# The two ends of a selective-scan layer: where its first rows wait and where its last projection stands

## The chip, the core and the metric

The program runs on one core of one Trainium2 chip. The metric is the device time of one execution in microseconds (us). The core's engines are named as the profile names them: PE (TensorE matmul), PEld (its weight loads), DVE (VectorE), ACT (ScalarE), POOL (GpSimd) and SP (SyncE, which here only issues DMAs). Each runs its own list of instructions in order and waits on the others by semaphores.

## The reference, cut to what matters

Four layers work on `x` of 3 x 256 x 48 x 48 (2304 tokens an image). Layer 0 holds attention, layers 1 and 2 are 3x3 convolutions, layer 3 is a selective scan along the tokens:

```python
# layer 3; b: image, l: token, d: 512 inner channels, n: 16 states
dt = softplus(x_dbl[..., :16] @ dt_proj_w.T + dt_proj_b)
def step(hst, inp):                       # one token
    dt_t, B_t, C_t, u_t = inp
    hst = hst * exp(dt_t[:, :, None] * A) + dt_t[:, :, None] * B_t[:, None, :] * u_t[:, :, None]
    return hst, einsum('bdn,bn->bd', hst, C_t)
y = (ys + u * D_param) * silu(z)
out = einsum('bld,cd->blc', y, out_proj_w)
x = x + out
```

The change touches the passage from layer 2 into layer 3 and the first and the last step of layer 3. What is computed stays the same.

## The kernel before

**Passage from layer 2.** Layers 1 and 2 work in half images (`halves`, twelve of them). A half's products of 3x3 kernels are L1546 (`ps_c`), and DVE writes their sums into `xs[b]`, the image in SBUF (L1573 to L1576). `store_tokens` (L1630) then copies a finished half into token order on ACT (L1642, two copies of 128 x 1152) into a staging tile, and one DMA (L1649) sends it to `xd[b]` in DRAM, whence layer 3 fetches it in chunks. For all halves but the last one the staging tile is `xpad` and SP issues the DMA. For the last, image 0's second half, it is a tile of the pool `vp` (`vt`) and ACT's queue issues it. Image 0 is last in `ORDER`, so layer 3 reads these tokens only in its last chunks. After the last half DVE also runs the group norm's last links (`norm_steps`, L180 to L192, L162, L216 to L218, L1614, L1615, with two small PE products and one POOL instruction between).

**Where layer 3's tiles lie.** When layer 2 ends, its pools are closed and layer 3's tiles take their places from the bottom up: first `wp` (five tiles of 6,144 bytes a partition, and `diag`), then `scn` in the order in which its tiles are first asked for: `dtr` (two buffers of 6,144), `dtur` (two of 3,104), `dtuq`, `hs` (three of 12,416), `hc` (two of 12,288). So `dtr` lies where the end of layer 2's weights (`u`, 36,864 bytes) and its product sums (`tmp`) were, and `hs` where `xpad`, `wc`, `we` and `vt` were. A tile's first use waits for what last used its place.

**The scan.** A chunk is 384 tokens of one image; there are 18. A chunk has eight steps (`m` in 0..3, `h` in 0..1), so there are 144 steps. A step has eight parts, and a part `(g, q)` is one ACT exponential of 128 x 384 (`decay`, L1809) into one of three PSUM slots and one DVE scan of 128 x 385 (`scan`, L1817) over a slice of the state tile `hs`. `decay` runs three parts ahead of `scan`. The scan's inputs are written into `hs` by `fill`: the upper half (q 0, 1) by DVE from the PSUM tile `ps_r` (`fill_upper`, L1765), which PE makes from `dtu` (`spread_pe`, L1730); the lower half (q 2, 3) by POOL (L1783, and one part by L1779) from rows that DMAs replicate (`dtur`, `dtuq`; `spread`, L1714, and `spread_second`, L1722). The rows that `decay` reads (`dtr`) come by `spread` as well. `fill(0)` writes step 0's upper half and a part of step 1's. After the eight parts of step s follow `fill(s+1)`, POOL's product with C over all of `hs` (`times_c`, L1834, result `hc`), and PE's sum over states of the step before (`add_states(s-1)`, L1851, with one product of `diag` and `u` at L1846 when h is 0). For the last step DVE makes the product with C in two halves (L1828).

**What stands beside the parts.** `run(at, j, place)` calls the other stages of the chunks before and after at fixed parts: `project_x` (L1263) for the next chunk after part 3 of step 0, `take_x` (L1269) on ACT at parts 5 and 6, `taps` (L1273, sixteen PE instructions for two m) at parts 6 and 7, `take_u` (L1281) on ACT in step 1. `gate` (L1858, DVE) multiplies a finished `y` with silu(z), three steps late. `project_y` is the output projection: one product of `ident` and the residual `ot` (L1372) and four of `w("out")` and `sz` (L1374) for each half of the channels. `store` copies it out of PSUM on ACT (L1384) and sends it (L1385).

**Busywork.** `keep_busy(src, times)` (L1333) issues that many PE products of 128 x 128 x 128 (L1336, two instructions each) whose results nobody reads, into the unused columns of the current `ps_r` tile. The table `busy` names the parts that get some, none of them in steps with m = 0 or m = 1.

**Order.** `keep_order` fixes the order of PE, DVE, ACT and POOL from `mark` on as the code has it. SP's order, and the order of what stands ahead of `mark`, come from the planner that places ready instructions.

After the last step the code of before does the whole of the last chunk's output: `residual`, `project_y` for m 0 to 2, `add_states(end)`, `gate`, `project_y` for m = 3 and `store`, for each half of the channels.

Of the kernel before, what the change touches and what calls it, by code (L numbers as in the profile page):

```python
# [9 lines left out]
F32 = mybir.dt.float32  # L10
# [6 lines left out]
P = 128  # L17
# [3 lines left out]
CT = 2  # L21
# [4 lines left out]
CH = 384  # L26
NCH = N // CH
NT = N // P
TW = HW // 4

PW = TW + 1
HR = HW // 2
HN = HR * TW
TAPS = 9
EXPERTS = 8
DI = 4
# [37 lines left out]
ORDER = (2, 1, 0)  # L74
# [10 lines left out]
def net(  # L85
# [21 lines left out]
    nc = tc.nc  # L107
# [44 lines left out]
    xs = {}  # L152
# [3 lines left out]
    xd = [dram.tile([P, CT, N], F32, name=f"xd{b}", bufs=1) for b in range(B)]  # L156
# [224 lines left out]
    with ExitStack() as l0:  # L381
# [36 lines left out]
        with ExitStack() as p1:  # L418
# [15 lines left out]
            for b in ORDER:  # L434
# [3 lines left out]
                for ct in range(CT):  # L438
                    for j in range(parts):
                        at = slice(j * N // parts, (j + 1) * N // parts)  # L440
                        queue = nc.scalar if b == ORDER[0] and ct else nc.sync
# [93 lines left out]
        with ExitStack() as p2:  # L535
# [9 lines left out]
            for i in range(NB):  # L545
# [399 lines left out]
                vt = vpool.tile([P, NT, 384], F32, name="vt")  # L945
# [101 lines left out]
        i = NB - 1  # L1047
        mark = listed[-1]
        chunks = [(b, c) for b in ORDER for c in range(NCH)]
# [15 lines left out]
        for n, b in enumerate(ORDER):  # L1065
# [11 lines left out]
            for c in range(NCH):  # L1077
# [7 lines left out]
                if b == 0 and c == 3:  # L1085
                    vp = late_pool("vp", 2, last_pools)
                    pad = late_pool("pad", stack=last_pools)
# [20 lines left out]
    rooms, w3v, chunks, stored = {}, {}, {}, set()  # L1108
# [224 lines left out]
    def keep_busy(src, times):  # L1333

        for i in range(times if spread_tiles else 0):
            nc.tensor.matmul(  # L1336
                spread_tiles[-1][:, i % 2, CH:], ident, src, start=True, stop=True
            )
# [30 lines left out]
    def project_y(k, mo, lo=0, hi=DI, into=None):  # L1369
        if lo == 0:  # L1370
            k.y_out[mo] = bank[mo] if into is None else into
            nc.tensor.matmul(k.y_out[mo], ident, k.ot[:, mo, :], start=True, stop=False)  # L1372
        for m in range(lo, hi):
            nc.tensor.matmul(  # L1374
                k.y_out[mo], w("out", m * 256 + mo * P, P), k.sz[:, m, :],
                start=False, stop=m == DI - 1,
            )

    def residual(k):
        k.ot = room(k, "ot")  # L1380
        nc.sync.dma_start(k.ot, xd[k.b][:, :, k.c * CH : (k.c + 1) * CH])

    def store(k, mo):
        nc.scalar.copy(k.ot[:, mo, :], k.y_out[mo])  # L1384
        nc.sync.dma_start(  # L1385
            out[k.b, mo * P : (mo + 1) * P, k.c * CH : (k.c + 1) * CH], k.ot[:, mo, :]
        )
# [148 lines left out]
    with ExitStack() as l1:  # L1536
# [88 lines left out]
        def between():  # L1625
            next(pending, None)
            if at_unit >= 4:
                next(early, None)

        def store_tokens(b, h):  # L1630


            last = (b, h) == (ORDER[-1], 1)
            if last:
                t = vp.tile([P, 6, CT, (HR + 2) * TW], F32, name="vt")
                t = t.rearrange("p i t n -> p (i t n)")
            else:
                t = pad.tile([P, 4, CT * (HR + 2) * PW + 2], F32, name="xpad")
                t = t.rearrange("p j n -> p (j n)")
            t = t[:, : CT * 4 * HN].rearrange("p (t n) -> p t n", t=CT)  # L1640
            for ct in range(CT):
                nc.scalar.copy(  # L1642
                    t[:, ct, :].rearrange("p (n j) -> p j n", j=4),
                    xs[b][:, ct, :].rearrange("p (j n) -> p j n", j=4)[
                        :, :, h * HN : (h + 1) * HN
                    ],
                )
            queue = nc.scalar if last else nc.sync
            queue.dma_start(xd[b][:, :, h * 4 * HN : (h + 1) * 4 * HN], t)  # L1649
            stored.add((b, h))  # L1650

        vt = first_v
        behind, pending = None, iter(())
        for n, (k, h) in enumerate(halves):
            layer, b = units[k]
# [13 lines left out]
            vt = ahead  # L1669
# [9 lines left out]
            pass  # L1679
        for _ in early:  # L1680
            pass

    last_pools.close()

# [4 lines left out]
    with ExitStack() as l3:  # L1689
# [2 lines left out]
        psr = l3.enter_context(tc.tile_pool(name="psr", bufs=1, space=PSUM))  # L1692
        psy = l3.enter_context(tc.tile_pool(name="psy", bufs=1, space=PSUM))

        scn = l3.enter_context(tc.tile_pool(name="scn", bufs=2, reuse_waits="tile"))
        for name in ("u", "dtu", "bc0", "bc1", "sz"):
            rooms[name].append(wp.tile([P, 4, CH], F32, name=name))
# [19 lines left out]
        def spread_second(k, m):  # L1717

            t = scn.tile([P, 4 + CH], F32, name="dtuq", bufs=1)[:, 2 : 2 + CH]
            for i in range(4):  # L1720
                r = slice(32 * i, 32 * i + 32)
                nc.sync.dma_start(t[r], k.dtud[m & 2][:32, m & 1, :])  # L1722
            k.second[m] = t

        def spread_pe(k, m):

            t = psr.tile([P, 2, 512], F32, name="ps_r")
            for q in range(2):
                r = slice(32 * q, 32 * q + 32)
                nc.tensor.matmul(  # L1730
                    t[:, q, :CH], rep[r].rearrange("p r d -> p (r d)"), k.dtu[r, m, :],
                    start=True, stop=True,
                )
            k.ps = t
            lent[0] = t[:, 1, :CH]
            spread_tiles[:] = [t]


        steps = [(at, m, h) for at in range(len(todo)) for m in range(DI) for h in range(2)]
        tiles = {}  # L1740
        state = {}
        busy = {(2, 0, 3): 4, (2, 1, 1): 3, (2, 1, 2): 3, (2, 1, 3): 3, (2, 1, 5): 3,
                (3, 0, 0): 3, (3, 0, 1): 3, (3, 0, 2): 2}
# [77 lines left out]
        def times_c(s):  # L1821
            at, m, h = steps[s]
            cb = chunks[at].bc[1][:, 2 * h : 2 * h + 2, :].unsqueeze(2)
            hc = scn.tile([P, 2, 4, CH], F32, name="hc")
            if s == len(steps) - 1:

                for g in range(2):
                    nc.vector.tensor_tensor(  # L1828
                        hc[:, g], tiles[s][:, g, :, 1:],
                        cb[:, g].broadcast_to([P, 4, CH]), ALU.mult,  # L1830
                    )
                tiles[s] = hc
                return
            nc.gpsimd.tensor_tensor(  # L1834
                hc, tiles[s][:, :, :, 1:], cb.broadcast_to([P, 2, 4, CH]), ALU.mult
            )
            tiles[s] = hc
# [18 lines left out]
        def gate(at, m):  # L1856
            k = chunks[at]
            nc.vector.tensor_tensor(k.sz[:, m, :], k.y_ps[:, :CH], k.sz[:, m, :], ALU.mult)  # L1858

        mark = listed[-1]  # L1860
        last = len(todo) - 1
        k = chunks[0]
        k.rows = {0: spread(k, 0)}
        spread_second(k, 0)
        spread_pe(k, 0)
        first_states(0)
        fill(0)
# [2 lines left out]
        for s, (at, m, h) in enumerate(steps):  # L1870
            if m == 0 and h == 1 and at + 2 <= last:
                fetch(at + 2)
            for part in range(8):
                j = 4 * m + 2 * h + part // 4
                scan(s, part)
                decay(8 * s + part + 3)
                if (m, h, part) in busy:
                    g, q = parts_of_step[part]
                    keep_busy(tiles[s][:, g, q, 1 : P + 1], busy[m, h, part])
                if part == 0 and h == 0:  # L1880
                    c, n = (at, m + 1) if m + 1 < DI else (at + 1, 0)
                    if c <= last:
                        rows = getattr(chunks[c], "rows", {})
                        chunks[c].rows = {**rows, n: spread(chunks[c], n)}
                if part == 0 and h == 1 and s + 1 < len(steps):
                    spread_second(chunks[steps[s + 1][0]], steps[s + 1][1])
                if part == 4 and s + 1 < len(steps):
                    first_states(s + 1)
                if part % 4 == 0:
                    run(at, j, BEGIN)  # L1890
                if part % 4 == 1:
                    run(at, j, MID)
                if part % 4 == 2:
                    run(at, j, DONE)
                if h == 1 and part == 7 and s >= 3:
                    gate(*steps[s - 3][:2])
                if part % 4 == 3:
                    run(at, j, LATE)
                if part == 3:
                    run(at, j, PE_)  # L1900
            if s + 1 < len(steps):
                fill(s + 1)
            last_states(s)
            times_c(s)
            run(at, 4 * m + 2 * h + 1, PE_)
            if s >= 1:
                add_states(s - 1)

            if h == 0 and s + 2 < len(steps):
                spread_pe(chunks[steps[s + 2][0]], steps[s + 2][1])  # L1910

        end = len(steps) - 1
        k = chunks[last]
        residual(k)
        for mo in range(2):
            project_y(k, mo, 0, DI - 1)
        add_states(end)
        gate(*steps[end][:2])
        for mo in range(2):
            project_y(k, mo, DI - 1, DI)  # L1920
            store(k, mo)
        keep_order(tc, listed, mark)
    late_pools.close()

# [111 lines left out]
```

## Time and profile before

| | us |
|---|---|
| median of the runs (3373.8 to 3378.72) | 3374.56 |
| the profiled execution's own time | 3369.03 |
| its span, first to last instruction | 3367.3 |
| layer 3's scans, first start to last end | 2013.78 to 3344.6 |
| DVE busy in the span | 2899.6 (86%) |
| PE busy | 3151.7 (94%) |
| ACT busy | 2375.1 (71%) |
| POOL busy | 1335.3 (40%) |

The page averages over four layers with different limits, so the stretches around 2000 to 2035 us and 3330 to 3367 us, which the change touches, are to be read by themselves in the timeline. A line of the timeline gives start, duration, engine, line, operation and tiles; in brackets stands the engine's idle time before it and what ended it. PE's busy time is modelled and is not PE at its peak. "PEclk" is the TensorE clock that was granted, as a share of full speed; it was 0.982 over the span and is either 1 or 0.5 in any stretch that is short enough.

### The profile page before, as it was taken

How to read it: one execution, taken by the hardware profiler on the slowest of the kernel's cores; microseconds unless marked ns; L12 is line 12 of the kernel's file. 1: busy time of each engine (PE TensorE's matmuls, PEld its weight loads, DVE VectorE, ACT ScalarE, POOL GpSimd, SP SyncE). 2: the span in 40 equal slices, each digit the busy share in tenths (PEclk: the TensorE clock that was granted, in tenths of full speed). 3: DMA queues.
4: the chain of work that ended last, by engine and by line, in shares of the span. 5: the costliest groups of instructions: out<-in, count | busy, mean ns of one | idle time of the engine just before them, and what ended most of it. 6: DMA issues, size and time to landing. Idle time of an engine off the chain costs nothing.

```text
span 3367.3 us, 54979 instructions
## 1 busy us (share of the span) xinstructions
PE 3151.7 (94%) x21314; PEld 1586.5 (47%) x21314; DVE 2899.6 (86%) x3302; ACT 2375.1 (71%) x3596; POOL 1335.3 (40%) x457
## 2 busy tenths in 40 slices
PE   7999999999999999979999988999999999999985
PEld 4334343452333434547777764444444444444442
DVE  4799989959988997379976459999999999999997
ACT  3688888838888886332233548888888888888874
POOL 0000000000000000220000009999999999999997
PEclk9999999999999999989999999999999999999998
DMA  4000000010000002566611044555545555555552
GB/s 174 23 8 10 8 8 6 8 46 4 8 7 8 10 8 71 193 210 214 218 38 38 19 120 107 125 127 129 143 123 141 133 129 123 130 130 134 135 131 56
DMA packets 182165, 290.84 MB, mean 86 GB/s; under 512 B 34738, under 2 KB 148466, under 8 KB 179971
## 3 DMA queue, kind: packets, MB, share of 16 engines
q1 hardware_dynamic: 168658, 267.15, 29.6%
q10 hardware_dynamic: 13232, 20.06, 1.8%
q8 instruction: 169, 2.77, 0.4%
q14 instruction: 106, 0.86, 0.1%
HBM read 236.24 MB, written 50.64 MB: 85 GB/s over the span
## 4 chain that ended last, share of the span: by engine, by line
PE 52%; DVE 32%; ACT 7%; DMA 4%; issue 4%; SPq 1%; POOL 0%; ACTq 0%; DVEq 0%; POOLq 0%
DVE hs L1817 21%; PE ps_s L638 16%; PE acc L651 14%; PE ps_c L1546 8%; DVE hs L1765 3%; DVE u L296 2%; PE ps_y L462 2%; PE ps_m L665 2%; ACT ps_da L1809 2%; PE ps_s L1031 2%; PE ps_m L711 1%; PE acc L529 1%; PE ps_s L518 1%; DVE ps_g L1343 1%; DMA dtr<-dtd 1%
## 5 line engine op out<-in xcount | busy, mean ns | idle before, releaser
L642 ACT ACTIVATE pt<-ps_s 128x1024 f32<-128x1024 f32 x972 | 942.4, 1022 | 154.8 <-PE ps_s L638 142.1
L1817 DVE TENSOR_TENSOR_SCAN hs<-ps_da,hs 128x385 f32<-128x385 f32 x1152 | 1002.6, 936 | 5.1 <-ACT ps_da L1809 2.4
L857 DVE TENSOR_TENSOR part<-part,pt 128x2048 f32<-128x2048 f32 x396 | 906.6, 2289 | 41.2 <-ACT pt L642 18.5
L1809 ACT ACTIVATE ps_da<-dtr,u 128x384 f32<-128x384 f32 x1152 | 656.3, 582 | 191.3 <-DVE hs L1817 182.7
L164 POOL TENSOR_TENSOR rstd<-ve,mhalf 128x2 f32<-128x2 f32 (+1 forms) x26 | 16.3, 629 | 1473.4 <-DVE ve L162 1473.4
L638 PE MATMUL ps_s<-q,kt 32*128 32x512 f32 (+1 forms) x4320 | 576.4, 592 | 0.1
L651 PE MATMUL acc<-pt,vt 128*32 128x512 f32 (+1 forms) x4320 | 520.9, 561 | 0.2
L1546 PE MATMUL ps_c<-vt,u 128*128 128x288 f32 x1728 | 429.4, 409 | 21.0 <-DVE u L263 21.0
L1834 POOL TENSOR_TENSOR hc<-hs,x 128x3072 f32<-128x3072 f32 x72 | 405.2, 5628 | 30.8 <-DVE hs L1817 26.0
L1834 POOL TENSOR_TENSOR hc<-hs,bc 128x3072 f32<-128x3072 f32 x71 | 400.1, 5635 | 24.7 <-DVE hs L1817 23.0
L1546 PEld LDWEIGHTS ps_c<-vt,u 128*128 128x128 f32 x1728 | 328.9, 191 | 116.6 <-issue 19.8
L638 PEld LDWEIGHTS ps_s<-q,kt 32*128 32x128 f32 x4320 | 195.3, 183 | 199.1 <-issue 120.2
L651 PEld LDWEIGHTS acc<-pt,vt 128*32 128x32 f32 x4320 | 94.4, 108 | 353.4 <-issue 326.7
L1851 PE MATMUL ps_y<-hc,u 128*32 128x384 f32 x2304 | 228.1, 516 | 2.8 <-POOL hc L1834 2.8
L1273 PE MATMUL ps_g<-u 128*128 128x384 f32 x576 | 196.2, 494 | 23.4 <-ACT u L1269 23.4
L1783 POOL TENSOR_TENSOR hs<-dtur,x 128x1536 f32<-128x1536 f32 x72 | 209.0, 2903 | 8.3 <-DMA dtur<-dtud 8.3
L1783 POOL TENSOR_TENSOR hs<-dtur,bc 128x1536 f32<-128x1536 f32 x72 | 209.3, 2907 | 1.3 <-DMA dtuq<-dtud 0.9
L1273 PEld LDWEIGHTS ps_g<-u 128*128 128x128 f32 x576 | 108.8, 191 | 107.7 <-ACT u L1269 34.6
L1336 PE MATMUL ps_r<-hs,ident 128*128 128x128 f32 x864 | 130.9, 292 | 27.3 <-DVE hs L1817 27.2
L1336 PEld LDWEIGHTS ps_r<-hs,ident 128*128 128x128 f32 x864 | 107.6, 192 | 80.8 <-DVE hs L1817 63.0
L1851 PEld LDWEIGHTS ps_y<-hc,u 128*32 128x32 f32 x2304 | 62.0, 112 | 144.5 <-issue 130.4
L1562 ACT COPY cb<-ps_c 128x288 f32<-128x288 f32 x48 | 19.1, 398 | 154.5 <-PE ps_c L1546 140.4
(266 smaller groups left out, 4051.0 us busy)
## 6 DMA issues: line engine op xcount, KB each, us to landing
wconv<-in_we SPq DMA_DIRECT2D x144, 384.0 KB, 4.2
dtr<-dtd SPq DMA_DIRECT2D x288, 192.0 KB, 3.9
dtur<-dtud SPq DMA_DIRECT2D x288, 96.0 KB, 4.3
wconv<-xd SPq DMA_DIRECT2D x36, 384.0 KB, 3.7
x<-bcd SPq DMA_DIRECT2D x72, 192.0 KB, 5.1
dtd<-x SPq DMA_DIRECT2D x36, 384.0 KB, 2.9
dtuq<-dtud SPq DMA_DIRECT2D x288, 48.0 KB, 2.0
bc<-bcd SPq DMA_DIRECT2D x72, 192.0 KB, 4.8
```

Source lines behind the costliest of these rows:

```text
L638: nc.tensor.matmul(s[:, j, cols], kt[r, mt * P : (mt + 1) * P], q[r, :n], start=True, stop=True,)
L642: nc.scalar.activation(p[:, h0 : h0 + 2, :], s, AF.Exp)
L651: nc.tensor.matmul(acc[h * HD : (h + 1) * HD, :n], vt[:, mt, g * P + h * HD : g * P + (h + 1) * HD], p[:, h, cols], start=mt == 0, stop=mt ...
L857: ): nc.vector.tensor_tensor(part, first, p, ALU.add)
L1273: nc.tensor.matmul(bank[m % 2], w3v["taps"][:, m, tap, :], w3v["xi"][:, m % 3, tap : tap + CH], start=tap == 0, stop=tap == DCONV - 1,)
L1336: nc.tensor.matmul(spread_tiles[-1][:, i % 2, CH:], ident, src, start=True, stop=True)
L1546: nc.tensor.matmul(pc[:, :HN], u[:, i, dy, ct, m * P : (m + 1) * P], vt[:, i, ct, dy * TW : dy * TW + HN], start=ct == 0 and dy == 0, stop ...
L1783: nc.gpsimd.tensor_tensor(states(s)[:, :, 2:4, 1:], chunks[at].rows[m][1].unsqueeze(1).broadcast_to([P, 2, 2, CH]), b_rows(s, 0, 2), ALU.mult,
L1809: nc.scalar.activation(slots[n % 3][:, 1 : CH + 1], chunks[at].rows[m][0][:, q, :], AF.Exp, scale=amat[:, col : col + 1],)
L1817: nc.vector.tensor_tensor_scan(b, slots[(8 * s + part) % 3][:, : CH + 1], b, 0.0, ALU.mult, ALU.add)
L1834: nc.gpsimd.tensor_tensor(hc, tiles[s][:, :, :, 1:], cb.broadcast_to([P, 2, 4, CH]), ALU.mult)
L1851: nc.tensor.matmul(k.y_ps[32 * q : 32 * q + 32, :CH], fold, hc[:, g, q, :], start=False, stop=h == 1 and g == 1,)
```

## The change

Six edits, all in layer 3 and in the passage into it:

- The last half's tokens are copied on ACT in four pieces (768, 384, 384 and 768 elements a partition) into the rooms `ot` (two) and `sq`, which the scan needs only later. Four DMAs on SP send them, placed in the code after `spread(k, 0)` and `spread_second(k, 0)` of the first chunk. The staging tile in `vp` and the DMA on ACT's queue are gone.
- `hc` gets a pool of its own, `hcp`, opened ahead of `scn`. By the sizes above, `hc` then lies over layer 2's `tmp` and the end of `u`, `dtr` and `dtur` over `xpad`, `wc`, `we` and the first `vt`, and `hs` over the two `vt` and image 0 (`x0`).
- Step 0 gets three `keep_busy` products in each of parts 1 to 4; the last step gets three in each of parts 4 to 7.
- In the last step `project_y` for m = 0, 1 stands at part 0, `gate` of m = 2 and `project_y` of m = 2 at part 3 (the gate stood at part 7 before); `residual` stands at part 0 of the step before.
- After the last step only `add_states`, `gate` and `project_y` of m = 3 remain, and both stores.
- The second store's copy runs on DVE, the first one's stays on ACT.

```diff
-    def store(k, mo):
-        nc.scalar.copy(k.ot[:, mo, :], k.y_out[mo])
+    def store(k, mo, copy=nc.scalar.copy):
+        copy(k.ot[:, mo, :], k.y_out[mo])
...
+        late_stores = []
+
         def store_tokens(b, h):
-            last = (b, h) == (ORDER[-1], 1)
-            if last:
-                t = vp.tile([P, 6, CT, (HR + 2) * TW], F32, name="vt")
-                t = t.rearrange("p i t n -> p (i t n)")
-            else:
-                t = pad.tile([P, 4, CT * (HR + 2) * PW + 2], F32, name="xpad")
-                t = t.rearrange("p j n -> p (j n)")
+            if (b, h) == (ORDER[-1], 1):
+                a, c = rooms["ot"]
+                d = rooms["sq"][0]
+                at = h * HN
+                for ct, lo, hi, t in (
+                    (0, 0, 192, a.rearrange("p t n -> p (t n)")),
+                    (0, 192, HN, c[:, 0, :]),
+                    (1, 0, 96, c[:, 1, :]),
+                    (1, 96, HN, d.rearrange("p t n -> p (t n)")),
+                ):
+                    nc.scalar.copy(
+                        t.rearrange("p (n j) -> p j n", j=4),
+                        xs[b][:, ct, :].rearrange("p (j n) -> p j n", j=4)[
+                            :, :, at + lo : at + hi
+                        ],
+                    )
+                    late_stores.append((xd[b][:, ct, 4 * (at + lo) : 4 * (at + hi)], t))
+                return
+            t = pad.tile([P, 4, CT * (HR + 2) * PW + 2], F32, name="xpad")
+            t = t.rearrange("p j n -> p (j n)")
...
-            queue = nc.scalar if last else nc.sync
-            queue.dma_start(xd[b][:, :, h * 4 * HN : (h + 1) * 4 * HN], t)
+            nc.sync.dma_start(xd[b][:, :, h * 4 * HN : (h + 1) * 4 * HN], t)
...
+        hcp = l3.enter_context(tc.tile_pool(name="hcp", bufs=2, reuse_waits="tile"))
         scn = l3.enter_context(tc.tile_pool(name="scn", bufs=2, reuse_waits="tile"))
...
-            hc = scn.tile([P, 2, 4, CH], F32, name="hc")
+            hc = hcp.tile([P, 2, 4, CH], F32, name="hc")
...
+        end = len(steps) - 1
         k = chunks[0]
         k.rows = {0: spread(k, 0)}
         spread_second(k, 0)
+        for dst, src in late_stores:
+            nc.sync.dma_start(dst, src)
         spread_pe(k, 0)
         first_states(0)
         fill(0)
...
-                if (m, h, part) in busy:
+                n = busy.get((m, h, part), 0)
+                if (s == 0 and 1 <= part <= 4) or (s == end and part >= 4):
+                    n = 3
+                if n:
                     g, q = parts_of_step[part]
-                    keep_busy(tiles[s][:, g, q, 1 : P + 1], busy[m, h, part])
+                    keep_busy(tiles[s][:, g, q, 1 : P + 1], n)
+                if s == end and part == 0:
+                    for mo in range(2):
+                        project_y(chunks[at], mo, 0, 2)
+                if s == end and part == 3:
+                    gate(at, DI - 2)
+                    for mo in range(2):
+                        project_y(chunks[at], mo, 2, DI - 1)
+                if s == end - 1 and part == 0:
+                    residual(chunks[at])
...
-                if h == 1 and part == 7 and s >= 3:
+                if h == 1 and part == 7 and 3 <= s < end:
                     gate(*steps[s - 3][:2])
...
-        end = len(steps) - 1
         k = chunks[last]
-        residual(k)
-        for mo in range(2):
-            project_y(k, mo, 0, DI - 1)
         add_states(end)
         gate(*steps[end][:2])
         for mo in range(2):
             project_y(k, mo, DI - 1, DI)
-            store(k, mo)
+        for mo in range(2):
+            store(k, mo, (nc.scalar.copy, nc.vector.tensor_copy)[mo])
```

More of the change, by code (lines that the diff above doesn't have):

```diff
@@ L1681, in net @@
             pass
+        stored.add((ORDER[-1], 1))
     last_pools.close()
```

## The prediction

> **What bounds the kernel now.** I read the page first, then the timeline around the first and the last scan, then the clock in windows. In layer 3, the last third of the span, DVE sets the pace:
>
> ```profile
> L1817 DVE TENSOR_TENSOR_SCAN hs<-ps_da,hs 128x385 f32<-128x385 f32 x1152 | 1002.6, 936 | 5.1 <-ACT ps_da L1809 2.4
> ...
> L1834 POOL TENSOR_TENSOR hc<-hs,x 128x3072 f32<-128x3072 f32 x72 | 405.2, 5628 | 30.8 <-DVE hs L1817 26.0
> ```
>
> The scans idle 5.1 us in all, so a step that starts earlier stays earlier: what is won at the first step should reach the end. From the first scan at 2013.78 to the last one's end at 3344.56 a step takes 1330.8 / 144 = 9.24 us. In the middle, then, there is nothing to win; the two ends are read by themselves. The first (timeline):
>
> ```profile
> 2005.17 7.97 SPq L1714 DMA_DIRECT2D dtur<-dtud  x4
> ...
> 2006.08 0.60 ACTq L1649 DMA_DIRECT2D xd<-vt  x1
> ...
> 2008.33 1.76 DVE L1765 TENSOR_TENSOR hs<-ps_r,x 128x1536 f32<-128x1536 f32 x1
> 2009.15 1.28 ACT L1809 ACT_TABLE_LOAD   x1 [2.23 <-DMA dtr<-dtd]
> ...
> 2012.91 0.96 DVE L1765 TENSOR_TENSOR hs<-ps_r,x 128x768 f32<-128x768 f32 x1 [2.82 <-DMA xd<-vt]
> ...
> 2018.10 3.51 DVE L1817 TENSOR_TENSOR_SCAN hs<-ps_da,hs 128x385 f32<-128x385 f32 x4 [0.82 <-POOL hs L1783]
> ...
> 2020.99 8.08 PE L1273 MATMUL ps_g<-u 128*128 128x384 f32 x16 [12.79 <-ACT u L1269]
> ...
> 2030.20 0.96 DVE L1817 TENSOR_TENSOR_SCAN hs<-ps_da,hs 128x385 f32<-128x385 f32 x1 [1.64 <-ACT ps_da L1809]
> ```
>
> To be seen: DVE and the fourth `dtur` issue wait until the staged tokens have landed (2012.8); ACT waits for `dtr`, POOL for `dtur`. Then `taps` run 8.08 us on a slow PE, ACT's `take_u` stands behind them, `decay` behind `take_u`, and step 1's last scan waits 1.64 us. Step 1 ends at 2031.16. The other end:
>
> ```profile
> 3336.64 2.39 PE L1851 MATMUL ps_y<-hc,u 128*32 128x384 f32 x16 [2.82 <-POOL hc L1834]
> ...
> 3344.93 4.21 DVE L1828 TENSOR_TENSOR hc<-hs,bc 128x1536 f32<-128x1536 f32 x2
> ...
> 3346.64 2.79 PE L1851 MATMUL ps_y<-hc,u 128*32 128x384 f32 x16
> ...
> 3349.36 1.58 PE L1372 MATMUL ps_g<-wconv,ident 128*128 128x384 f32 x2
> ...
> 3356.96 0.56 DVE L1858 TENSOR_TENSOR sz<-ps_y,sz 128x384 f32<-128x384 f32 x1 [7.82 <-PE ps_y L1851]
> ```
>
> DVE is done at 3349.14; PE alone holds the end until 3356.96. And the clock, in windows (busy us and instructions of PE, PEld, DVE, ACT, POOL; then PEclk, the DMA share, GB/s):
>
> ```profile
> 2013.80:2021.00 7.20, 0.01 (x1) 0.01 (x1) 6.38 (x9) 4.11 (x9) 5.84 (x3) 0.50 0.81 196
> 2021.00:2026.30 5.30, 5.30 (x9) 2.88 (x10) 5.30 (x8) 3.19 (x7) 5.29 (x2) 0.50 0.20 48
> ...
> 3339.10:3345.00 5.90, 0.00 (x0) 0.00 (x0) 5.90 (x9) 2.47 (x5) 5.90 (x2) 0.50 0.00 1
> 3345.00:3350.70 5.70, 5.63 (x20) 1.94 (x21) 4.14 (x3) 0.00 (x0) 0.85 (x1) 0.50 0.01 3
> 3350.70:3357.00 6.30, 6.19 (x31) 2.89 (x29) 0.04 (x1) 0.00 (x0) 0.00 (x0) 1.00 0.00 0
> ```
>
> PE idles ahead of both ends and then works 5.3 and 5.7 us at half clock.
>
> [...]
>
> **Part by part, the start.** The two ACT copies took 2.27 us each. The first half's run beside the products, as now. Behind the last sum (2003.75) stand two pieces, 384 and 768: 2.27 plus one more start, for which I take the 0.19 of the eight-element copy L1792: to 2006.2. ACT then has L1792 (0.2), the table load (1.28) and one exponential (0.58): 2008.4 at the earliest for scan 0, if `dtr` is there. By the tile sizes `dtr` no longer lies over weights that PE reads to 2003.3 but over tiles free since about 1978, and its source was stored at 1971: SP can issue it behind the stores of 1987, some 15 us ahead of need. That cover hides all twelve row DMAs; without it their landing (3 to 5 us) is back. DVE has the norm's links to 2008.23 and the two fills: 2008.33 + 1.67 + 0.9 = 2010.9. If the planner puts the fills into the norm chain's gaps, the links end at about 2010.2 instead. I take **scan 0 at 2010.3**, bounds 2008.4 and 2010.9. POOL has its rows and is done before part 4, so the 0.82 us go too.
>
> SP gets four issues of 0.56 us (2.2 us) in place of ACT's one. Queued behind them are the rows of m = 1; the fourth `dtur` issue above shows that an issue also waits for the landing of a DMA some issues back. The 1.18 MB landed 6.7 us after their issue; so these rows are in by 2017, and step 2 wants them at about 2023: 6 us of cover, cost nothing. The rooms `ot` and `sq` are wanted tens of us later.
>
> The busywork of step 0 is not free. In PE's fixed order parts 1 to 3 now stand ahead of `project_x`, which ran at 2005 to 2008 before, and part 4 behind it. It writes the `ps_r` tile which the next `fill_upper` reads, so DVE waits for it. PE will be idle for some 5 us before part 1's scan ends (t0 = scan 0 + 1.7), hence cold. Eighteen instructions at 0.22 to 0.26 (weight loads and products of the eight at 3316.89): 4.3 us. `project_x`, eight of 0.36 warm or 0.64 cold; [...]3.0. Part 4, six of 0.15: 0.9. DVE may fill at t0 + 8.2, then 0.45 and eight scans, 6.9. Step 1 ends at 2010.3 + 1.7 + 8.2 + 0.45 + 6.9 = 2027.55. `taps`, sixteen warm ones of 0.325, end at t0 + 13.4, `take_u` and `decay` by 14.6; the last scan is due at 14.7, so the stalls of 0.43 and 1.64 go. Gain 2031.16 - 2027.55 = **3.6 us**. Bounds: late clock and late fills 2.2; scan 0 at 2008.4 and PE warm (t0 + 6.5) 7.2.
>
> **The end**, in times of before. PE takes up `project_y` for m = 0, 1 right after 3339.03: twelve instructions. If the clock fell as it did, [...]2.3 cold ones and 9.7 of 0.325, to 3343.65. The gate (0.45) at part 3 needs only the sum done at 3339.03 and moves within DVE's list. Then four instructions (1.3), busywork 24 x 0.15 = 3.6, to 3348.55; L1846 0.7 and L1851 1.45, to 3350.7; last sum 1.45: the gate at 3352.15, a gain of 4.8. Warm throughout, PE is ready at 3349.1, DVE's product at 3349.2: 3350.6, a gain of 6.35. [...]I take **5.4 us**. Lower bound, clock back only at 3343.9: the gate at 3353.8, 3.15. `residual`'s DMA was issued at 3321.48 already; it costs nothing. The tail of 3367.3 - 3356.96 = 10.34 us stays: DVE's copy is taken at L1858's 0.53 against ACT's 0.48, either way within 0.1.
>
> **Sum.** 3.6 + 5.4 = 9.0 us. The profiled execution took 3369.03 (1.7 around its span): 3360.0. The median, 5.5 above it, should move alike: 3374.56 - 9.0 = **3365.6**.
>
> **Rivals.**
> - *Both ends warm*, the fills early: 7.2 + 6.35 = 13.5, 3361.1. For it: bigger pieces of PE work. Against: 5 us of idling ahead of step 0. 0.10.
> - *PE takes the gain back*: busywork and `project_x` hold the fill, the clock returns late at both ends: 2.2 + 3.15 = 5.35, 3369.2. For it: the cold stretches above. [...]0.18.
> - *It doesn't do what it says*: SP has the four stores ahead of the first rows. Last copy 2006.2, issues to 2008.5, `dtr` to 2010.2, 1.95 MB at the window's 220 GB/s in by 2016, table and exponential: scan 0 at 2017.9, a loss of 4.0; with 5.4: 3373.2. Against: the code has them behind. 0.05.
> - *Slower: POOL becomes the bound.* Two steps hold two L1834 (5.63), two L1783 (2.90) and one L1779 (0.87): 17.93 us of 18.48. The moved tiles must not slow it: from 3.8% on (18.60, 9.0 / 72 more) the gain is gone. At 5%: 0.35 x 72 = 25 lost, 3390.6. Against: `hc<-hs,x` and `hc<-hs,bc` read other places at 5628 and 5635 ns. 0.07.
>
> **Numbers.** The likeliest case has 0.60 and 3363 to 3368.5; 0.03 of it fall short of 0.2% (6.75 us), about what a measurement of this kernel can tell from no change. Faster: 0.57 + 0.10 = 0.67. Same: 0.03 + 0.18 + 0.05 = 0.26. Slower: 0.07. The range runs from the first rival's 3361 to 3371.5, which takes in the second's 3369.2 and the median's own spread.
>
> **What would show it.** Right: `dtr` landed before 2004 (in times of before), no wait on a landing at the fills, scan 0 near 2010; a short DVE wait on PE's L1336 at step 0's end; no `decay` wait at step 1's; the gate 1 to 3 us after L1828's end in place of 7.8. Wrong: `dtr` behind the stores on SP, L1834 above 5.7 us, or a step above 9.24.

## The result, and the profile after

The changed kernel takes **3367.38 us** (median of 13 runs, 3360.95 to 3370.64), the kernel before 3373.43 (13 runs, 3368.78 to 3378.72): ratio 0.9979, interval 0.9971 to 0.9987, so some 7 us or 0.2% faster (the interval allows 4.4 to 9.8 us; the two medians are 6.1 apart). 3365.6 had been forecast.

The two profiled executions took 3369.03 and 3367.55 us, only 1.5 apart, because they are not alike ahead of the change. The last sum of layer 2 (L1576, the last DVE work before the first scan that both kernels do in the same way) starts at 2003.29 before and at 2009.76 after. Of these 6.5 us, 3.5 are there 70 us into the program and 6.3 at 1682 us, while the first instruction that the change alters is an ACT copy near 1984. So this lateness is not the change's. At its largest step PE runs at half clock in one profile and at full clock in the other (the same window, before and then after; busy us and instructions of PE, PEld, DVE, ACT, POOL, then PEclk, the DMA share, GB/s):

```profile
43.00:49.80 6.80, 6.80 (x28) 4.32 (x27) 0.32 (x2) 3.13 (x5) 0.00 (x0) 1.00 1.00 362
```

```profile
43.00:49.80 6.80, 6.80 (x18) 4.38 (x17) 0.32 (x2) 1.34 (x2) 0.00 (x0) 0.50 1.01 372
```

The profiled execution of before lay 4.4 us under its kernel's median, that of after at its median. In what follows each time is therefore counted from the start of that last sum ("+"), and the end from the start of the last step. The trace then shows where the gain is:

| us | before | after | forecast |
|---|---|---|---|
| scan 0 | +10.50 | +9.88 | +7.0 |
| end of step 0 | +18.32 | +16.79 | |
| end of step 1 | +27.87 | +26.91 | +24.3 |
| steps 2 to 142, start to start | 1304.08 | 1304.20 | as before |
| last gate, from the start of the last step | 19.29 | 12.03 | 13.9 |
| from that gate to the end | 10.33 | 10.48 | as before |
| from the last sum to the end | 1364.00 | 1356.06 | 1355.0 |

So 7.3 of the 7.9 us come from the end and 1.0 from the start, and the tail and the middle take 0.3 back. The 1.0 is not secured: the kernel with the end's edits alone, further down, has the start of before and ends step 1 at +26.47, 1.4 us earlier than the profile of before. The middle passes on what the start wins: POOL's product, which one rival wanted slower, is what it was, and the scans idle 5.2 us in all against 5.1 (page, costliest groups).

```profile
L1833 DVE TENSOR_TENSOR_SCAN hs<-ps_da,hs 128x385 f32<-128x385 f32 x1152 | 1002.1, 935 | 5.2 <-ACT ps_da L1825 3.7
...
L1850 POOL TENSOR_TENSOR hc<-hs,x 128x3072 f32<-128x3072 f32 x72 | 405.3, 5630 | 32.1 <-DVE hs L1833 28.2
```

The start after (timeline; start, duration, and in brackets the idle time before and what ended it):

```profile
1993.46 1.63 SPq L1883 DMA_DIRECT2D xd<-wconv  x2
...
2011.17 0.32 SPq L1883 DMA_DIRECT2D xd<-wconv  x1
...
2011.59 1.80 SPq L1730 DMA_DIRECT2D dtr<-dtd  x4
2011.62 1.76 DVE L1781 TENSOR_TENSOR hs<-ps_r,x 128x1536 f32<-128x1536 f32 x1
...
2016.40 0.17 DVE L216 COPY gsc<-rstd 128x2 f32<-128x2 f32 x1 [0.80 <-POOL rstd L164]
...
2017.73 1.28 ACT L1825 ACT_TABLE_LOAD   x1 [5.19 <-DMA dtr<-dtd]
...
2019.64 6.91 DVE L1833 TENSOR_TENSOR_SCAN hs<-ps_da,hs 128x385 f32<-128x385 f32 x8 [2.80 <-ACT ps_da L1825]
...
2021.51 4.21 PE L1336 MATMUL ps_r<-hs,ident 128*128 128x128 f32 x18 [6.10 <-DVE hs L1833]
...
2025.51 3.09 PE L1263 MATMUL ps_g<-u 128*128 128x387 f32 x8
...
2028.43 0.83 PE L1336 MATMUL ps_r<-hs,ident 128*128 128x128 f32 x6
...
2029.10 5.33 PE L1273 MATMUL ps_g<-u 128*128 128x384 f32 x16
2029.30 0.56 DVE L1781 TENSOR_TENSOR hs<-ps_r,x 128x384 f32<-128x384 f32 x1 [2.75 <-PE ps_r L1336]
...
2029.78 6.89 DVE L1833 TENSOR_TENSOR_SCAN hs<-ps_da,hs 128x385 f32<-128x385 f32 x8
```

Read it from SP down. The planner puts two late stores early, but the third one, which waits for ACT's copy of the last half, stands ahead of the rows: `dtr` is issued only behind it, at 2011.59, lands 6.1 us later, and ACT waits 5.19 us for it. DVE is ready 2.8 us before the first scan. Then the added busywork does what was forecast of it, for good and ill: `taps` take 5.33 us in place of 8.08 and step 1 has no stall left, but DVE waits 2.75 us for PE's L1336 at the fill ahead of it.

The end after:

```profile
3341.87 1.50 PE L1867 MATMUL ps_y<-hc,u 128*32 128x384 f32 x16 [2.38 <-POOL hc L1850]
...
3343.30 0.91 PE L1372 MATMUL ps_g<-wconv,ident 128*128 128x384 f32 x2
...
3348.69 2.96 PE L1336 MATMUL ps_r<-hs,ident 128*128 128x128 f32 x24
...
3350.59 3.78 DVE L1844 TENSOR_TENSOR hc<-hs,bc 128x1536 f32<-128x1536 f32 x2
...
3351.49 0.81 PE L1862 MATMUL ps_y<-u,diag 128*128 128x384 f32 x2
...
3352.23 3.04 PE L1867 MATMUL ps_y<-hc,u 128*32 128x384 f32 x32
...
3355.34 0.56 DVE L1874 TENSOR_TENSOR sz<-ps_y,sz 128x384 f32<-128x384 f32 x1 [0.97 <-PE ps_y L1867]
```

The gate comes 0.97 us after the end of DVE's product, where it came 7.82 after it before: the projection (L1372, L1374), which PE did ahead of its last sum then, is out of the way, and DVE's product, not PE, is last.

### The profile page after: what moved, and what is told of

The parts are those of the page before. It is cut to its first block, busy times and chain, and to the rows that moved or that the text cites. A ratio compares the mean times of both kernels' runs of the same rounds, so it can differ in the third digit from the quotient of the medians.

```text
span 3365.8 us, 55074 instructions
## 1 busy us (share of the span) xinstructions
PE 3162.3 (94%) x21362; PEld 1595.9 (47%) x21362; DVE 2899.7 (86%) x3303; ACT 2375.1 (71%) x3597; POOL 1334.2 (40%) x457
## 4 chain that ended last, share of the span: by engine, by line
PE 52%; DVE 31%; ACT 7%; DMA 5%; issue 4%; SPq 1%; POOL 0%; ACTq 0%; DVEq 0%; POOLq 0%
DVE hs L1833 21%; PE ps_s L638 16%; PE acc L651 14%; PE ps_c L1546 9%; DVE hs L1781 3%; PE ps_s L1031 2%; PE ps_y L462 2%; ACT ps_da L1825 1%; PE ps_m L665 1%; DVE u L296 1%; PE ps_m L711 1%; PE acc L529 1%; DMA dtr<-dtd 1%; PE ps_s L518 1%; DVE ps_g L1343 1%
## 5 line engine op out<-in xcount | busy, mean ns | idle before, releaser
L1850 POOL TENSOR_TENSOR hc<-hs,x 128x3072 f32<-128x3072 f32 x72 | 405.3, 5630 | 32.1 <-DVE hs L1833 28.2
L1850 POOL TENSOR_TENSOR hc<-hs,bc 128x3072 f32<-128x3072 f32 x71 | 399.7, 5629 | 25.4 <-DVE hs L1833 22.5
L1336 PE MATMUL ps_r<-hs,ident 128*128 128x128 f32 x912 | 138.1, 294 | 30.5 <-DVE hs L1833 30.4
L1336 PEld LDWEIGHTS ps_r<-hs,ident 128*128 128x128 f32 x912 | 114.6, 194 | 84.4 <-DVE hs L1833 66.1
```

The costliest lines, as they stand in the source:

```text
L1336: nc.tensor.matmul(spread_tiles[-1][:, i % 2, CH:], ident, src, start=True, stop=True)
L1850: nc.gpsimd.tensor_tensor(hc, tiles[s][:, :, :, 1:], cb.broadcast_to([P, 2, 4, CH]), ALU.mult)
```

## The experiments

Theory at the outset: the gain is the end's; the start gives little because SP has the rows behind a late store, and because the busywork costs at the fill what it saves in `taps`. The rivals stand in the expectations. All kernels were timed in rounds beside the kernel before on the same chip; where two versions are compared with each other, the trace says more than the intervals, which are 4 to 6 us wide (9 us for the two kernels with only five runs). A trace is one execution, though: differences of about 1 us at the start are within what the same code shows there (step 1 ends at +27.87 in the profile of before, at +26.47 in the next kernel).

**The end alone.** The kernel before with the edits of the end (projection and gate in the last step, its busywork, `residual` earlier, both stores last, the second one's copy on DVE).

> The kernel before with the edits of the end alone (projection inside the last step, busywork in its parts 4 to 7, the second store on DVE). Theory A (the end is by itself worth 7.2 us, DVE's product being its limit): from the last step's first scan to the last gate 12.0 us instead of 19.3, ratio to before 0.9979. Theory B (part of it comes from the new places or from a lucky clock): 13.5 to 15, ratio 0.9984 to 0.9988.

Measured: 3367.26 us, ratio 0.9982 (0.9976 to 0.9989). The gate comes 13.10 us into the last step, between the numbers of the two theories (a slow PE, see below). By its time the end alone has nearly the whole gain, 6.1 of 7.1 us. From the last sum to the end it takes 1355.90, 8.1 less than before, but that is too much credit: 1.4 us of it arise at the start, which is the code of before. There `taps` took 6.99 us in place of 8.08. In the profile of before the granted clock is 0.50 up to 2026.38, for the first 5.4 us of `taps`, and at full clock (from 2037.04) the same sixteen instructions take 5.43; by its duration, then, less of this `taps` was at half clock:

```profile
2021.58 6.99 PE L1273 MATMUL ps_g<-u 128*128 128x384 f32 x16 [12.49 <-ACT u L1269]
```

The edits of the end were not tried one by one, apart from the busywork below; that the projection's place is what counts is read from the traces.

**The start alone.** The kernel before with late stores, `hcp` and step 0's busywork.

> The changed kernel with the end as it was before. Theory A (the start gains next to nothing since the rows stand behind a store and the busywork holds the fill): step 1 ends 26.9 us after the last sum's start against 27.9 before; ratio to before 0.9997. Theory B (the start gains the forecast 3.6 us and the profile of the changed kernel was an odd one): ratio 0.9989.

Measured: 3372.01 us, ratio 0.9998 (0.9990 to 1.0007). Step 1 ends at +27.05 (before +27.87, the end alone +26.47). By its time it can't be told from no change, as theory A has it.

**No busywork in step 0.**

```diff
-                if (s == 0 and 1 <= part <= 4) or (s == end and part >= 4):
+                if s == end and part >= 4:
```

> The changed kernel without the busywork of step 0. Theory A (the busywork costs at the fill what it saves at the taps): project_x runs ahead of the scans again, the 2.75 us in which DVE waits for PE go, the taps run cold and stall the last scans of step 1 by about 2.1; step 1 ends 26.4 us after the last sum's start instead of 26.9, the time is within 1 us of the changed kernel's. Theory B (the busywork is what gains at the start): step 1 ends at 28.5 to 29, the time is 2 us longer than the changed kernel's.

Measured: 3365.92 us, ratio 0.9976 (0.9970 to 0.9983). The wait at the fill is gone, the stalls of 2.1 us in step 1 are back, and step 1 ends at +25.97, 0.9 earlier than with it (+26.91). So as theory A has it, this busywork saves nothing here; it costs a little more than it saves.

**The rows first.** The late stores are held behind the last of the twelve row DMAs in SP's order:

```diff
+        rows_end = listed[-1].name
         for dst, src in late_stores:
             nc.sync.dma_start(dst, src)
+            tc.add_manual_dep(
+                listed[-1], rows_end,
+                mybir.DependencyInfo(mybir.DependencyClass.NoSync, mybir.DependencyReason.DATA),
+                reason="order",
+            )
```

> The changed kernel, with its four late stores made to stand behind the first chunk's twelve row DMAs on SP. Theory A (SP's order: the first rows stood behind the third late store, which waits for the last sum's ACT copy): the rows are issued some 10 us before layer 2's last sum, ACT no longer waits for dtr, scan 0 starts 7.1 us after the last sum's start instead of 9.9, step 1 ends at 24.1 instead of 26.9, and the time falls by 2.8 us against the changed kernel (ratio to before about 0.9970). Theory B (the rows were held by their own tiles' places or by the DMA engines' load, not by the queue): scan 0 stays at 9.9, ratio stays at 0.9979.

Measured: 3366.6 us, ratio 0.9981 (0.9974 to 0.9987). The rows were issued from 1991.3 to 1998.5 and the first decays were done at 2013.2 (+5.7). Yet scan 0 starts at +10.31. So SP's order was one of two holds, and theory A's number fell. The timeline of DVE, then of POOL, names the second one:

```profile
2013.17 0.16 DVE L162 TENSOR_SCALAR ve<-ps_gv 128x2 f32<-128x2 f32 x1 [0.68 <-PE ps_gv L195]
2014.13 2.86 DVE L216 COPY gsc<-rstd 128x2 f32<-128x2 f32 x1 [0.80 <-POOL rstd L164]
2016.91 0.15 DVE L218 SCALAR_TENSOR_TENSOR gsh<-gm,rstd 128x2 f32<-128x2 f32 x1
2017.03 0.79 DVE L1614 COPY norm<-gsc 128x2 f32<-128x2 f32 x1
...
2017.80 6.90 DVE L1833 TENSOR_TENSOR_SCAN hs<-ps_da,hs 128x385 f32<-128x385 f32 x8
```

```profile
2014.06 2.91 POOL L1799 TENSOR_TENSOR hs<-dtur,x 128x1536 f32<-128x1536 f32 x1
2016.93 0.86 POOL L1795 TENSOR_TENSOR hs<-dtuq,x 128x384 f32<-128x384 f32 x1
```

A copy of two elements a partition takes 2.86 us; it starts 0.07 after POOL's product and ends with it, and so does the second copy with POOL's next one. In the changed kernel, where POOL had no row yet, the same copies took 0.17 (2016.40 above). With the rows early, POOL simply got there first. The traces show when the copies end, not what in POOL's products holds them. In this trace the fill of step 1 waits 2.94 us for the busywork as before.

New theory: three things hold the start one behind the other, the rows' place on SP, POOL's products ahead of the copies, and the busywork ahead of `project_x` in PE's order. The next runs take them away in turn.

**Rows first, projection first.** As the last one, and `project_x` stands at part 0 of step 0, ahead of the busywork:

```diff
+                if s == 0 and part == 0:
+                    run(at, 0, PE_)
...
-                if part == 3:
+                if part == 3 and s:
```

> The changed kernel with the rows of the first chunk ahead of the four late stores on SP, and with the input projection of step 0 issued to PE ahead of the added busywork. Theory A (with the rows early, [...]VectorE's three small copies of the norm chain wait for GpSimd's products; and what holds the fill of the second step is the busywork ahead of the projections in PE's queue): scan 0 still 10.3 us after the start of the last sum, but the wait of about 2.9 us at that fill is gone, so step 1 ends near +24.6 against 26.9 for the changed kernel; time 2 us below the changed kernel's. Theory B (the fill waits for PE's clock and the projection itself, wherever the busywork stands): the wait stays between 2 and 3 us, step 1 ends near +27, time as the changed kernel's.

Measured: 3364.32 us, ratio 0.9978 (0.9970 to 0.9986). Scan 0 at +10.10, L216 again 2.86 us, the wait at the fill 0.43, the end of step 1 at +24.80. As theory A has it, the wait at the fill goes (2.94 to 0.43), and step 1 ends 2.1 us earlier than in the changed kernel; the interval of the time is too wide to show them.

**And no small copies on DVE.** What is tried is whether POOL's products are what held the copies. POOL writes the factor straight to its place and multiplies the shift:

```diff
+        out = None
+        if pool:
+            out = small.tile([P, CT], F32, name="gsc", bufs=4), small.tile([P, 2], F32, name="rstd")
...
+        if out is not None:
+            nc.vector.tensor_scalar(out[1], ps[:, :n], -1.0, None, ALU.mult)
...
+        if pool:
+            sh = small.tile([P, CT], F32, name="gsh", bufs=4)
+            nc.gpsimd.tensor_tensor(sh, out[1], rstd, ALU.mult)
+            return mv, rstd, sh
```

> The kernel with rows first and projection first, and with VectorE's three small copies at the end of the last norm taken away: GpSimd writes the factor straight to its place and multiplies the shift itself (one more product of 128x2), VectorE only negates the mean earlier. Theory A ([...]): VectorE has nothing to wait for, scan 0 starts at about +5.9, when the first decays are there; the fifth part waits until GpSimd's product for the upper rows is done at about +10.2, step 0 ends near +13.7 and step 1 near +21.8; time about 5 us below the changed kernel's, ratio to the kernel before near 0.9965. Theory B (scan 0 at +10.3 was held by something else, GpSimd's own product being needed by it): scan 0 stays at or above +9.5 and the time is that of the kernel with rows and projection first.

Measured: **3360.97 us, ratio 0.9963 (0.9950 to 0.9976)**. Its timeline, DVE and then POOL:

```profile
2014.00 0.16 DVE L162 TENSOR_SCALAR ve<-ps_gv 128x2 f32<-128x2 f32 x1 [0.48 <-PE ps_gv L198]
2014.07 3.50 DVE L1845 TENSOR_TENSOR_SCAN hs<-ps_da,hs 128x385 f32<-128x385 f32 x4
2018.18 3.51 DVE L1845 TENSOR_TENSOR_SCAN hs<-ps_da,hs 128x385 f32<-128x385 f32 x4 [0.61 <-POOL hs L1811]
2021.61 0.53 DVE L1793 TENSOR_TENSOR hs<-ps_r,x 128x384 f32<-128x384 f32 x1
2022.06 7.01 DVE L1845 TENSOR_TENSOR_SCAN hs<-ps_da,hs 128x385 f32<-128x385 f32 x8
```

```profile
2015.00 0.20 POOL L223 TENSOR_TENSOR gsh<-rstd,gsc 128x2 f32<-128x2 f32 x1
2015.25 2.90 POOL L1811 TENSOR_TENSOR hs<-dtur,x 128x1536 f32<-128x1536 f32 x1
```

The last sum starts at 2008.52, so scan 0 comes at +5.55 (forecast +5.9), step 0 ends at +13.17 (+13.7), step 1 at +20.56 (+21.8). The scans run beside POOL's product and are not held as the copies were: four take 3.50 us, and in the kernel with the rows first alone eight take 6.90, with POOL idle from 2020.65 on. Of the 4.55 us by which scan 0 comes earlier than in the last kernel, 3.3 are what the two held copies took too long; the rest is the links that DVE no longer does and its wait for POOL's factor. From the last sum to the end it takes 1350.72 us, 5.3 less than the changed kernel. There are only five runs, and the interval overlaps the changed kernel's a little; a second kernel with this start, below, has the same time.

**Rows first, no busywork in step 0.**

> The changed kernel with the rows ahead of the late stores and without the busywork in step 0. Theory A (busywork at the start saves in the taps what it costs at the fill): scan 0 at +10.3, no wait at the fill, the taps stall step 1 as in the kernel before, step 1 ends at +26 to +27; time that of the changed kernel. Theory B (the busywork is a gain by itself): step 1 ends later than with it, near +29, and the time is 2 us above the changed kernel's.

Measured: 3365.57 us, ratio 0.9976 (0.9967 to 0.9985). Scan 0 at +10.10, step 1 ends at +25.78: neither +26 to +27 nor +29, but 1.0 later than with the busywork behind the projection (+24.80), and 1.7 earlier than with it ahead of the projection (+27.51). In both kernels of the +24.80 and the +25.78 `project_x` ran early (from +1.83), so in effect they differ by the busywork alone. In these profiles, then, it is worth 1 us, in the right place only; by the times it can't be told from nothing.

**The end's busywork.** First the changed kernel without it:

```diff
-                if (s == 0 and 1 <= part <= 4) or (s == end and part >= 4):
+                if s == 0 and 1 <= part <= 4:
```

> The changed kernel without the busywork in the parts 4 to 7 of the last step. Theory A (VectorE's product is the limit at the end, PE only if it is slow): if PE's clock falls, the second part of the output projection takes about 6 us in place of 3 and the gate starts at about +13.7 in place of +12.0; time 1 to 2 us above the changed kernel's. Theory B (VectorE's product sets the end whatever PE's clock is): gate at +12.0 to +12.3 and the same time as the changed kernel, so that this busywork is worth nothing.

Measured: 3364.7 us, ratio 0.9978 (0.9970 to 0.9987), the gate at 12.03 as with it. PE stayed at full clock without it (the sixteen instructions at the start of the last step took 1.50 us), so theory A, which speaks of a slow PE, was not tried. Three kernels (the end alone, and the two without busywork in step 0) had the gate at 13.10 to 13.17, with a slow PE at the start of the last step (L1372 took 1.19 to 1.65 us in place of 0.91). So, to meet a slow PE, both kinds of busywork were taken out:

> The changed kernel without any of its added busywork, at the start or at the end. The kernels without the busywork of step 0 had their last gate at +13.1 to +13.2, with PE at a low clock at the start of the last step and 2.84 us of busywork after that, in place of +12.0. Theory A (the gate at +13.1 is PE being late by that busywork, which VectorE's product would otherwise cover): gate at +12.0 and time 0.5 to 1.5 us below the changed kernel's. Theory B (PE is late by its clock alone, and without busywork the last products run at the low clock): gate at +13.1 or later and time that of the changed kernel or more.

Measured: 3365.76 us, ratio 0.9979 (0.9973 to 0.9986), the gate at 12.03. PE's own timeline, first of the kernel without busywork in step 0 but with it at the end, then of this one:

```profile
3337.16 1.62 PE L1867 MATMUL ps_y<-hc,u 128*32 128x384 f32 x16 [2.41 <-POOL hc L1850]
3338.71 1.65 PE L1372 MATMUL ps_g<-wconv,ident 128*128 128x384 f32 x2
3340.15 2.29 PE L1374 MATMUL ps_g<-sz,u 128*128 128x384 f32 x4
...
3345.50 2.84 PE L1336 MATMUL ps_r<-hs,ident 128*128 128x128 f32 x24
3348.18 0.81 PE L1862 MATMUL ps_y<-u,diag 128*128 128x384 f32 x2
3348.92 2.79 PE L1867 MATMUL ps_y<-hc,u 128*32 128x384 f32 x32
```

```profile
3338.97 1.65 PE L1372 MATMUL ps_g<-wconv,ident 128*128 128x384 f32 x2
3340.41 2.31 PE L1374 MATMUL ps_g<-sz,u 128*128 128x384 f32 x4
...
3345.78 0.81 PE L1862 MATMUL ps_y<-u,diag 128*128 128x384 f32 x2
3346.72 2.47 PE L1867 MATMUL ps_y<-hc,u 128*32 128x384 f32 x24
3350.00 0.85 PE L1867 MATMUL ps_y<-hc,u 128*32 128x384 f32 x8 [0.82 <-DVE hc L1844]
```

Both start the step at the low clock (L1372 at 1.65 against 0.91). With 2.84 us of busywork PE is late and does the last 32 instructions in one run; without it PE is back in time, at full clock (its last eight take 0.85, 0.11 each, where the sixteen at 3346.64 took 0.17 each at half clock in the profile of before), and waits for DVE. So theory A holds for the gate; the time is too coarse to show it. At the end the busywork gains nothing where PE is at full clock (12.03 with and without it) and costs 1.1 us where it is not (13.10 to 13.17 against 12.03).

**The best start, without the end's busywork.**

> The version with rows first, projection first and no small copies on VectorE, and besides without the busywork of the last step. Theory A (the end waits for VectorE's product once PE is not late, so that busywork is worth nothing): gate at +12.0, time within 1 us of the version with the busywork, ratio to the kernel before near 0.9963. Theory B (the busywork keeps PE's clock where the start has changed): PE's last products take 6 us in place of 3, gate at +13.5 to +14.5, time 2 us more.

Measured: **3361.27 us, ratio 0.9961 (0.9948 to 0.9974)**, the gate at 12.04, the last sum to the end 1350.11. Here too PE began the last step at the low clock (the sixteen instructions of the sum before, L1879 here, took 2.79 us), and without busywork the gate is not late: theory A. The two versions with the mended start cannot be told apart by their time. Against the kernel without any busywork, timed in the same rounds, this one is 4.5 us faster (3361.27 and 3365.76).

**The place alone.** The kernel before with the pool `hcp` and nothing else.

> The kernel before with one edit: the products' buffers get a pool of their own, so that the dt rows lie where the last staging was, while the old staging and its single store stay. Theory A (the place is what joins the start to the staging): what writes into these rooms waits until the staged tokens have been stored and their transfer has landed, so scan 0 comes 2 to 4 us later than in the kernel before (+10.5), the time 2 to 4 us above it. Theory B (the place is worth nothing either way, other buffers hold the start already): scan 0 within 0.5 us of +10.5 and the same time.

Measured: 3372.76 us, ratio 1.0 (0.9992 to 1.0008), scan 0 at +10.28, step 1's end at +26.18. These are theory B's numbers. The wait is there as theory A has it, but it is one that other waits already covered:

```profile
2013.63 0.17 DVE L216 COPY gsc<-rstd 128x2 f32<-128x2 f32 x1 [0.80 <-POOL rstd L164]
...
2016.67 0.20 ACT L1793 COPY hs<-u 128x8 f32<-128x8 f32 x1 [4.77 <-DMA xd<-vt]
2016.89 2.62 DVE L1766 TENSOR_TENSOR hs<-ps_r,x 128x1536 f32<-128x1536 f32 x2 [2.81 <-ACT hs L1793]
```

POOL works its first row at 2020.47 only, and the copy takes 0.17 again.

## Why the prediction was right, and where it was not

- **The sum was right, its parts were not.** 9.0 us were forecast; the trace has 7.9 after the last sum, the runs 7.1. The start fell short by 2.6, the end gained 1.9 more than was put down. That these two errors nearly cancel is luck, and so in part is the end: with the low clock of three other kernels its gate would have come 1.1 later (13.10 to 13.17 there, 12.03 here).
- **The step that failed: "SP can issue it behind the stores of 1987, some 15 us ahead of need."** The tiles were free and the source stored: with the rows first, `dtr` is issued at 1991.31. But SP's order stands by the planner, and the planner put the third late store, which waits for ACT's copy behind the last sum, ahead of `dtr` (2011.59). The rival *It doesn't do what it says* had named this order, at 0.05, though with all four stores ahead; its price was too high (scan 0 at +14.6, measured +9.88), because only three stood there, two of them issued 18 us earlier.
- **It was not the only fault of that step.** With the rows early, scan 0 still came at +10.31, by DVE's copies held behind POOL's products. The forecast's +7.0 let every engine run by itself; "POOL has its rows and is done before part 4" did not ask what POOL would meet when it starts early. With rows and copies both mended the first scan came at +5.55, inside the forecast's bounds of +5.1 to +7.6.
- **The busywork of step 0 went as forecast.** From scan 0 to the end of step 1 17.25 us were forecast and 17.03 measured: L1336 4.3 against 4.21, `project_x` 3.0 against 3.09, the last six 0.9 against 0.83. The stalls of 0.43 and 1.64 went. But the forecast set only 0.1 us of its 3.6 on this chain (17.37 in the profile of before); the other 3.5 were to come from scan 0, which moved by 0.6. And the 17.37 was a slow case, 16.30 in the kernel with the end alone. What the chain could give it gave with `project_x` first: 14.7.
- **The end was mis-sized in two terms.** PE stayed at full clock at the start of the last step (its sixteen instructions took 1.50 us), where the forecast's 5.4 gives the low one a weight of 0.6 (0.6 x 4.8 + 0.4 x 6.35). That weight, and the times at which the clock was to return, were the author's estimates, not shown by a trace; the low clock came in 6 of the 9 kernels listed in the last section. And for a full clock the gate was put at 3350.6, 12.93 into the step, by adding 1.45 for the whole last sum behind DVE's product. Measured is 12.03: the gate comes 0.97 behind the product, since only eight of the 32 instructions are left then, and the product itself took 3.78 in place of 4.21. In the kernel before it ran beside POOL's L1834 for its first 0.9 us, after it beside L1850 for 0.5; whether that makes the difference was not tried by itself. Busywork was forecast at 3.6 and took 2.96, off the path.
- **POOL as the bound is out:** 5630 ns against 5628.
- **The tail** was put at no change: 10.48 against 10.34, and 9.97 to 11.52 over all kernels.
- **Two of its sums** are 0.1 off: the addends of the earliest scan 0 give 2008.3, and a scan 0 at 2017.9 loses 4.1. Nothing hangs on either.

What stays open: what in POOL's products holds the copies, and what the start is worth by time in the changed kernel, since 1 us is below what the runs can tell.

## What to carry to other kernels

A transfer that "can be issued early" is early only if nothing that waits stands ahead of it on its queue (`dtr`: 2011.59 in place of 1991.31): look at the issue order, not at the code's order. When work of another engine is made to start earlier, ask which small instructions it will meet; here two copies of two elements a partition took 3.65 us in place of 0.34. Busywork belongs behind the real work that others wait for, and where another engine sets the end it is worth nothing. One profile shows one course of PE's clock (`taps` took 8.08 and 6.99 us in two kernels with the same start): before a stall on a slow PE is priced, look at it in a second kernel that has the same code there.

## What the runs showed of the hardware

- A DVE copy of 128 x 2 in f32 takes 0.17 us (L216 in the profiles of before and after and in four other kernels, POOL idle), and 2.86 us when a POOL product of 2.90 to 2.91 us started 0.07 us ahead of it (rows first, with and without the projection first). Four scans take 3.50 us beside the same POOL product (no small copies on DVE).
- PE idled for 2.25 to 2.82 us ahead of the sixteen instructions that begin the last step. In the changed kernel, the same without the end's busywork, and the one with rows and projection first (pauses of 2.25 to 2.38) these took 1.50 us. In six others they took longer (pauses of 2.41 to 2.82): 2.16 to 2.79 us in the kernel before, the end alone, the rows first without busywork in step 0 and the best start without the end's busywork; 1.62 without busywork in step 0 and 1.59 without any. So a forecast that needed PE at full clock behind such a pause had two outcomes here; what decides between them was not shown.
- In the profiles of before and after the granted clock is 1 or 0.5 and its changes lie whole multiples of 3.41 us from one another (before: down at 2012.73, up at 2026.38, four of them; down at 3337.10, up at 3350.75, four). Before, it fell at 3337.10 behind 3.41 us in which PE was busy for 0.59. After, it stayed at 1 through the two such stretches from 3336.86, with PE busy for 2.62 and 1.82.
- PE's busy time alone does not tell when it falls, though: in layer 3 of the profile of before it fell six times behind 3.41 us in which PE was busy for 0.85 to 0.88 of the time.
